# Moving band loads between two DMA queues in a convolution and involution kernel: SyncE issues every eighth transfer of a band instead of every fourth

## The chip, the cores and the metric

The kernel runs on one core of a Trainium2 chip. The metric is the device time of one execution in microseconds (us); lower is better. The kernel before took 1477.5 us in the median of three runs (1473.41 to 1481.04).

## What is computed

The input `x` has 32 images of 256 channels and 32 x 32 pixels, in float32. Two residual layers follow each other. The first adds a 3 x 3 convolution, rounded to half precision, of the group-normalized input. The second adds an involution: every pixel gets its own 7 x 7 weights for each of 16 groups of channels.

```python
# layer 0
x = x + conv3x3_fp16(gn(x), L0_conv_weight) + L0_conv_bias
# layer 1, with xn = gn(x)
y = relu(bn(einsum('oc,bchw->bohw', w1, xn)))        # 256 -> 64 channels
w = einsum('oc,bchw->bohw', w2, y) + b2              # 64 -> 7*7*16 weights per pixel
w = w.reshape(b, 16, 49, 32, 32)
patches = all 7x7 shifts of the padded xn, as (b, 16, 16, 49, 32, 32)
out = einsum('bgkhw,bgckhw->bgchw', w, patches)
x = x + out.reshape(b, 256, 32, 32)
```

## The kernel before

The kernel goes image by image, in steps that one hand-written loop lays out: 16 steps per image, and at each step the loop emits some work of several images at different stages. The order in which an engine's instructions are emitted is the order in which it runs them. The order is the same for the queues of DMA transfers, which SyncE (SP) and GpSimd (POOL) issue.

An image passes these stages.

- `load_x` (L105, SP) brings the image in. `front` does the group norms on ScalarE (L210, L269), the 3 x 3 convolution on TensorE (L320), its addition on VectorE (L334, L336), the 256 to 64 reduction (L368, L375) and the transposed pixels (L383, L387).
- `weights` makes the involution weights of four image rows: TensorE multiplies into `pw` (L398), and VectorE adds the bias and writes the result into the ring `w_sb` (L416). The ring holds 24 rows (`RING`), so a row's place is written again 24 rows later, and VectorE then has to wait until the scatter of the old rows has read them.
- `scatter` (L465, SP) copies a band of eight rows out of `w_sb` into the scratch `wd` in HBM, as seven transfers of 160 KB, one for each horizontal shift.
- `load_bands` (L478) reads the same band back in another layout, into one of three SBUF buffers (`bands`, `NBAND`), as 16 transfers of 70.2 KB. Each fills eight partitions of the buffer.
- `sums` (L503) multiplies the band with the transposed pixels on TensorE, and `add_windows` (L519) adds the result to the image on VectorE. `store` (L524, SP) writes the image out.

An image has four bands (`K`), so there are 128 bands, 896 scatter transfers and 2048 band loads. In the step loop, the scatter of a band stands one or two bands' worth of steps ahead of its load, and the load stands nine steps ahead of its sums. Within a step the scatter is emitted before the band load. On SP's queue the order is therefore: scatter of band k+1, loads of band k, scatter of band k+2, loads of band k+1, and so on, with the image's two loads and two stores in between.

Each queue has eight semaphores in rotation. A transfer waits for the one that was issued eight places earlier on the same queue, besides what its data need: a scatter waits for VectorE's writes and for the loads of the band that last used its rows of `wd`; a band load waits for the scatter of its band and for the sums that last used its buffer.

Which queue issues which of a band's 16 loads is decided by this line and the constant `SHARE`:

```python
queue = nc.sync if i % SHARE == SHARE - 1 else nc.gpsimd
queue.dma_start(band[j::JC, :, j * WB : j * WB + WPIX], src)
```

With `SHARE = 4`, SP issues the loads 3, 7, 11 and 15 of a band, and POOL the other twelve. POOL has nothing else to do after the start.

Of the kernel before, what the change touches and what calls it, by code (L numbers as in the profile page):

```python
# [59 lines left out]
ROW = S * WPIX  # L60
WR = 4
NBAND = 3
SHARE = 4
NPIX = 6
RING = 24
FRONT = -56
# [5 lines left out]
def tile_quant_conv_then_involution(  # L72
# [394 lines left out]
    def load_bands(b, k):  # L467

        band = bands[(b * K + k) % NBAND]
        for i in range(JC):  # L470
# [5 lines left out]
            )  # L476
            queue = nc.sync if i % SHARE == SHARE - 1 else nc.gpsimd
            queue.dma_start(band[j::JC, :, j * WB : j * WB + WPIX], src)  # L478
# [136 lines left out]
```

## Time and profile before

| | |
|---|---|
| median of 3 runs | 1477.5 us |
| profiled execution | 1467.2 us |
| its span, first to last instruction | 1465.4 us |
| mean granted clock of TensorE | 0.961 |
| TensorE busy | 1296.1 us |
| VectorE busy | 931.2 us |
| GpSimd busy, issue of its transfers included | 863.6 us |
| ScalarE busy | 734.7 us |
| moved by DMA | 369.32 MB, 252 GB/s in the mean |

The profile is that of one execution, so its parts add up to that execution's time and not to the median. A row of the groups names the line, the engine, the operation and the tiles; then it gives the busy time and the mean of one instruction, and the idle time of the engine ahead of it with what ended that idle time. A row of the waits reads "engine line waited for <- releaser: us in total, times, longest us". SP and POOL appear as SPq and POOL where they issue transfers. Queue q1 is the one that SP fills, and q0 the one that POOL fills.

### The profile page before, as it was taken

To read this page: it belongs to the slowest core of one execution; us is meant where nothing else is said; L and a number is where in the kernel's file an instruction comes from. 1 tells how busy PE (TensorE), PEld (TensorE's weight loads), DVE (VectorE), ACT (ScalarE), POOL (GpSimd) and SP (SyncE) were. 2 spreads that over 40 slices of the span, in tenths; PEclk is the share of its full clock that TensorE was granted. 3 is DMA by queue.
4 is the path that set the end of the run, shared out by engine and by line. 5 is a ranking of instruction groups with operands and counts; after the bars stand their busy time and mean duration, and the time that the engine had idled before them with its cause. 6 is when DMAs were issued, how large, how long until landed. Compare 5 with 4: busy or idle time off the path is not lost.

```text
span 1465.4 us, 70178 instructions
## 1 busy us (share of the span) xinstructions
PE 1296.1 (88%) x29440; PEld 804.8 (55%) x29440; DVE 931.2 (64%) x3180; ACT 734.7 (50%) x1699; POOL 863.6 (59%) x1561
## 2 busy tenths in 40 slices
PE   4899989898989899889898989998999999899764
PEld 1455555565556565556565555565555555556553
DVE  4566666676666676666666656666666666666652
ACT  5865545554545545455554555554555545553300
POOL 6066656565655566555566556566655556566664
PEclk9999999999999999999999999999999999999886
DMA  6189999999999999999999999999999999999996
GB/s 205 23 229 272 259 261 271 262 269 249 266 256 259 265 263 265 263 256 259 262 265 249 262 261 263 258 263 256 263 268 260 260 266 265 265 264 252 271 262 194
DMA packets 360089, 369.32 MB, mean 252 GB/s; under 512 B 72480, under 2 KB 302048, under 8 KB 359520
## 3 DMA queue, kind: packets, MB, share of 16 engines
q1 hardware_dynamic: 286048, 254.14, 61.9%
q0 software_dynamic: 73728, 110.69, 28.6%
q8 instruction: 235, 3.85, 1.1%
q14 instruction: 78, 0.64, 0.1%
HBM read 183.81 MB, written 180.74 MB: 249 GB/s over the span
## 4 chain that ended last, share of the span: by engine, by line
PE 42%; DMA 30%; SPq 10%; DVE 8%; issue 5%; ACT 3%; POOL 2%; DVEq 0%; ACTq 0%; POOLq 0%
PE pc L320 18%; DMA wd<-w_sb 14%; DMA band<-wd 14%; PE acc L503 11%; PE pw L398 9%; SPq L465 8%; DVE w_sb L416 5%; PE py L368 3%; POOL band L478 2%; DMA out<-x 2%; PE pt L383 1%; SPq L478 1%; ACT junk L210 1%; DVE x L519 1%; DVE x L336 1%
## 5 line engine op out<-in xcount | busy, mean ns | idle before, releaser
L478 POOL DMA_DIRECT2D band<-wd x1536 | 838.2, 548 | 588.3 <-DMA band<-wd 405.1
L416 DVE TENSOR_TENSOR w_sb<-pw,b_sb 128x16 f32<-128x16 f32 (+9 forms) x1920 | 454.2, 349 | 446.9 <-PE pw L398 269.5
L320 PE MATMUL pc<-xq,wq 128*128 128x496 f16 (+3 forms) x2304 | 550.0, 386 | 28.7 <-ACT xq L269 21.4
L503 PE MATMUL acc<-band,pixels 64*32 64x190 f32 (+1 forms) x16384 | 414.1, 321 | 40.9 <-issue 14.7
L320 PEld LDWEIGHTS <-wq 128*128 128x128 f16 x2304 | 210.1, 100 | 338.5 <-issue 130.6
L398 PE MATMUL pw<-w_sb,y 64*32 64x224 f32 (+1 forms) x8192 | 313.8, 340 | 87.9 <-DVE w_sb L416 61.0
L503 PEld LDWEIGHTS acc<-band,pixels 64*32 64x32 f32 x16384 | 295.7, 107 | 126.6 <-issue 79.7
L519 DVE TENSOR_TENSOR x<-acc,x 128x380 f32<-128x380 f32 (+1 forms) x512 | 261.7, 511 | 33.1 <-PE acc L503 24.2
L398 PEld LDWEIGHTS pw<-w_sb,y 64*32 64x32 f32 x8192 | 182.9, 108 | 141.1 <-issue 115.5
L210 ACT ACTIVATE junk<-x 128x512 f16<-128x512 f32 (+1 forms) x192 | 146.8, 764 | 74.9 <-DVE x L336 69.6
L387 ACT COPY pixels<-pt 128x512 f32<-128x512 f32 x128 | 73.6, 575 | 193.7 <-PE pt L383 193.7
L210 ACT ACTIVATE junk<-x,mean 128x1024 f16<-128x1024 f32 x128 | 147.1, 1149 | 4.3
L241 ACT ACTIVATE s<-back,eps 128x2 f32<-128x2 f32 x64 | 18.9, 296 | 201.0 <-DVE back L226 200.9
L334 DVE TENSOR_SCALAR q<-pc 128x512 f16<-128x512 f32 x128 | 87.3, 682 | 16.9 <-PE pc L320 16.8
L269 ACT ACTIVATE xn<-x,off,rstd 128x512 f32<-128x512 f32 x128 | 96.1, 799 | 0.0
L336 DVE SCALAR_TENSOR_TENSOR x<-q,bias_sb,x 128x512 f32<-128x512 f16 x128 | 91.9, 718 | 0.2
L231 ACT ACTIVATE mean<-back 128x2 f32<-128x2 f32 x64 | 12.9, 202 | 143.1 <-DVE back L226 143.1
L383 PE MATMUL pt<-ident,xn 128*128 128x128 f32 x512 | 77.8, 275 | 3.5 <-ACT pixels L387 3.5
L383 PEld LDWEIGHTS pt<-ident,xn 128*128 128x128 f32 x512 | 63.8, 142 | 29.9 <-ACT pixels L387 4.4
L269 ACT ACTIVATE xq<-x,off,rstd 128x1024 f16<-128x1024 f32 x64 | 75.9, 1228 | 2.3 <-PE pc L320 2.3
L368 PEld LDWEIGHTS py<-xn,w_sb 128*64 128x64 f32 x2048 | 63.1, 138 | 18.9 <-issue 13.6
L368 PE MATMUL py<-xn,w_sb 128*64 128x64 f32 x2048 | 68.0, 224 | 3.2 <-ACT xn L269 1.8
(40 smaller groups left out, 370.7 us busy)
## 6 DMA issues: line engine op xcount, KB each, us to landing
wd<-w_sb SPq DMA_DIRECT2D x896, 160.0 KB
band<-wd POOLq DMA_DIRECT2D x1536, 70.2 KB
band<-wd SPq DMA_DIRECT2D x512, 70.2 KB
x<-in_x SPq DMA_DIRECT2D x64, 512.0 KB
out<-x SPq DMA_DIRECT2D x64, 512.0 KB
band<-in_w SPq DMA_DIRECT2D x2, 1152.0 KB
w_sb<-in_w SPq DMA_DIRECT2D x2, 196.0 KB
wd<-band SPq DMA_DIRECT2D x2, 180.0 KB
```

Source lines behind the costliest of these rows:

```text
L210: nc.scalar.activation(junk[:, n0:n1], src[:, h, n0:n1], func, bias=bias, accum_out=self.sums[:, i : i + 1])
L269: nc.scalar.activation(dst, src, AF.Identity, bias=self.off[:, one], scale=self.rstd[:, one])
L320: nc.tensor.matmul(pc.rearrange("p (r c) -> p r c", c=W)[:, r0 - nt * RT : r1 - nt * RT, c0:c1], wq[:, kh, k, mh * P : (mh + 1) * P], xq[: ...
L336: nc.vector.scalar_tensor_tensor(xt[:, mh, cols], q, bias_sb[:, mh : mh + 1], xt[:, mh, cols], ALU.add, ALU.add)
L368: nc.tensor.matmul(py[i * CR : (i + 1) * CR, cols], w1_sb[:, kh, :], px[:, r : r + 2], start=kh == 0, stop=kh == CH - 1,)
L383: nc.tensor.transpose(pt[:, i, h * P : (h + 1) * P], xn[:, h, (m + i) * P : (m + i + 1) * P], ident)
L398: nc.tensor.matmul(pws[i][t * TW : (t + 1) * TW, r, : dj.stop - dj.start], y_sb[b % 2][half, (r0 // 2 + r) * W : (r0 // 2 + r + 1) * W], w ...
L416: nc.vector.tensor_tensor(to, pws[i][:p, r : r + rows, e, d0 * G : d1 * G].rearrange("p r (d g) -> p r d g", g=G), b2_sb[:p, e, d0 * G : d ...
L465: nc.sync.dma_start(to, rows.rearrange("p s g r -> p s (g r)"))
L478: queue.dma_start(band[j::JC, :, j * WB : j * WB + WPIX], src)
L503: nc.tensor.matmul(at[t * TW : (t + 1) * TW, h, :, f - top : l - top], px[p, a, v * GC : v * GC + TW], of[:, :, 2 * a + v, f - top : l - top],
L519: nc.vector.tensor_tensor(x_at, of, x_at, ALU.add)
```

## The change

The constant is doubled, and nothing else is edited.

```diff
-SHARE = 4
+SHARE = 8
```

SP now issues the loads 7 and 15 of a band, and POOL the other fourteen. Over the 128 bands SP issues 256 band loads instead of 512, and POOL 1792 instead of 1536. The transfers themselves are the same: same source, same destination and same size.

## The prediction

> **What bounds the kernel now.** I read the page's part 1 and 2 first, then the queues, the chain, the waits of the steady part (130 to 1390 us), and last the order of time on SyncE's queue.
>
> ```profile
> PE 1296.1 (88%) x29440; PEld 804.8 (55%) x29440; DVE 931.2 (64%) x3180; ACT 734.7 (50%) x1699; POOL 863.6 (59%) x1561
> ...
> DMA  6189999999999999999999999999999999999996
> ...
> q1 hardware_dynamic: 286048, 254.14, 61.9%
> q0 software_dynamic: 73728, 110.69, 28.6%
> ...
> PE 42%; DMA 30%; SPq 10%; DVE 8%; issue 5%; ACT 3%; POOL 2%; DVEq 0%; ACTq 0%; POOLq 0%
> ```
>
> No engine is full: PE is busy 88% of the span and 1152.1 of the 1260 us between 130 and 1390, so it idles 107.9 us there. The transfer engines are at 0.95 in the same stretch, and the chain gives DMA and SP's queue 40% together. The waits of that stretch say where PE's idle time comes from:
>
> ```profile
> POOL band L478 <- DMA band<-wd: 379.8, 277, 9.5
> DVE w_sb L416 <- PE pw L398: 246.9, 176, 5.9
> ...
> DVE w_sb L416 <- DMA wd<-w_sb: 95.4, 19, 8.4
> ...
> DVE w_sb L416 <- DMA band<-wd: 64.7, 13, 7.2
> ...
> PE pw L398 <- DVE w_sb L416: 57.1, 42, 4.4
> POOL band L478 <- DMA wd<-w_sb: 54.4, 23, 6.2
> ...
> PE pw L398 <- issue: 25.4, 26, 2.2
> ```
>
> VectorE (L416) writes new weights into the ring w_sb and must first see that the scatter (L465) has taken the old ones out. 32 times, about once an image, it waits 5.0 us on average (95.4 + 64.7 = 160.1 us). By the instruction list the DMAs that L416 waits for are scatters only; the name band<-wd in the second row is that of the update that came last. PE then waits for VectorE: 57.1 us, the largest cause of its idle time. PE waits for a band itself only 13.2 us in the whole run.
>
> Why is the scatter late? SP's queue in order of time (start, length, instructions):
>
> ```profile
> 817.02 5.28 SPq L465 DMA_DIRECT2D wd<-w_sb  x7
> 822.41 2.68 SPq L478 DMA_DIRECT2D band<-wd  x4
> 825.45 5.02 SPq L465 DMA_DIRECT2D wd<-w_sb  x7
> 830.57 3.54 SPq L478 DMA_DIRECT2D band<-wd  x4
> 834.21 0.40 SPq L524 DMA_DIRECT2D out<-x  x1
> 834.97 6.04 SPq L465 DMA_DIRECT2D wd<-w_sb  x7
> 841.10 1.63 SPq L524 DMA_DIRECT2D out<-x  x1
> 842.83 2.72 SPq L478 DMA_DIRECT2D band<-wd  x4
> ```
>
> There is hardly a hole. Summed over 130 to 1390 us from the trace's records, SP spends 595.1 us issuing scatters (813, mean 732 ns), 332.7 us band loads (466, mean 714 ns), 70.9 us image loads and stores: 998.7 us, 79% of the stretch; most of the rest waits for a free slot, because each transfer waits for the one issued eight before it on the same queue. Pairing each scatter with the VectorE instruction that it waits for, I find that the scatter goes out 5.1 us (median) after its data are ready. So **SP's queue is late by its own issuing**, not for want of data.
>
> **What the Trainium skill says.** "DMA: Bandwidth & Descriptors", section "Issuing engines are not separate DMA queues": transfers of all issuers run on the same 16 engines, and spreading them saves only the time to initiate. The trace agrees that this time counts: 714 ns each on SP, 547 on POOL. Same page, "Why a DMA increments its semaphore by 16 and not by 1": a transfer whose outer dimension is 8 runs on 8 engines; from SP on the lowest eight, from POOL on eight chosen by a rotating cursor, and from POOL all 16 post. The trace agrees in part: a band load on SP shows one update about 1.0 us after its issue and eight more at 3.7 to 5.2 us, one on POOL shows 16; and the first scatter behind four band loads has eight of its updates within 0.36 us, the other eight spread out to 2.0 us. So SP's band loads do pile on one half of the engines; the cursor is not visible here. "SBUF — State Buffer", section "SBUF: two separate sides", warns that VectorE in some modes stops POOL from writing descriptors. This trace shows none of it: 1536 issues on POOL took 547 ns in the minimum and the median, 681 at most.
>
> **The change part by part.** Sizes, sources and waits for data stay; per band SP issues 2 loads instead of 4, POOL 14 instead of 12.
>
> (1) *Off SP:* 256 issues x 713 ns = 183 us, with the gaps ahead of them (72.6 us for 466 in the steady part, 0.156 us each) 256 x 0.87 = 222 us, or 7 us per image. This lies on the path: the next scatter stands right behind the loads. It comes 2 x 0.87 = 1.7 us earlier at once, and more as the queue stops carrying lateness over from band to band. I take 3 us of the 5.1 as recovered (bounds: 1.7 and 5.1). VectorE's wait of 5.0 us falls to 2.0, and PE's 57.1 us shrink in the same ratio: -57.1 x 3/5 = **-34 us** (bounds -19 and -57; with the 25.4 us of unexplained idle time at L398 -82).
>
> (2) *Onto POOL:* 256 x 547 ns = 140 us of issuing. POOL too has eight slots. Its 12 loads take 7.8 us from first to last issue (0.71 each), and it idles 2.5 us on average before the next band. 14 loads make 9.2 + 0.5 = 9.7 us plus about 0.2 us of start against a band period of 43.3/4 = 10.8 us: it still fits, at 92%. Scatters land unevenly, though (8.9, 9.1, 10.6 and 15.4 us apart), so the four bands of an image end later by about 1.7, 2.5, 4.2 and 2.9 us. The cover is the time between the last POOL landing and the start of the sums: medians 3.2, 3.7, 4.9 and 8.0 us. Subtracting band by band, PE would lose 1.04 us per image, 33 us in all, if the scatters came no earlier. But POOL starts 0.8 us after the scatter lands, so the 3 us of (1) go straight off its delays, leaving at most 1.2 us, inside the cover: I take **+2 us** (bounds 0 and +33).
>
> (3) *Engines of the DMA:* each moved load has 32 small packets of 10 ns instead of 8: 256 x 24 x 10 ns / 16 = 4 us of engine time; I take **+2 us**. Against it, SP's band packets hold 2002 us of engine time on eight engines, 250 us each. Half of it moved and spread evenly takes 125 - 62.5 = 62 us from the fuller eight. How much of it reaches the end the trace of before cannot show (bounds 0 and -62); I count 0 here, since it is partly the same gain as (1).
>
> (4) *SP's remaining waits:* scatter k waits for POOL's loads of band k-4 and POOL for the sums of band k-3 (12 us in all now, PE pt); both have room of ten us and more, so later POOL loads cost nothing there, unless POOL falls a whole band behind.
>
> Sum: -34 + 2 + 2 = -30 us. The profiled execution took 1467.2 us (span 1465.4 and 1.8 around it), so 1437, or 0.98 of it. The median of the three runs is 1477.5, 0.7% above the profiled one; I take the same 30 us from it: **1447**.
>
> **The rivals.**
> *A, POOL becomes the late queue (slower).* Place: L478 on POOL. At 14 loads per band it is 92% occupied, and a band that starts behind keeps the lateness until the 15 us gap of the fourth. It decides where the scatters land less than about 1 us earlier than now. Price: +33 us by (2), 1510. For it: POOL's 379.8 us of slot waits, the largest line. Against: POOL's rest of 2.5 us per band, and 5.1 us of lateness upstream that mends. 16%.
> *B, nothing moves (same).* The bytes are the same and the DMA engines are 0.95 busy; a queue that issues earlier only waits longer in the engines. For it: latencies of 5.2 to 5.9 us in both queues point to full engines. Against: periods per image vary from 39 to 47 us at the same bytes, and the engines' share falls to 0.92 in some stretches. 1470 to 1485; 14%.
> *C, the uneven halves are the true limit (faster by more).* Then the whole 62 us of (3) come off: 1415. For it: the eight late updates behind the band loads. Against: PE, 91% busy in the steady part, could not follow all the way. 15%.
> That the change doesn't do what it says is excluded: the instruction lists of the two kernels differ by the queue of these 256 loads and, following from it, in which earlier transfer a later one on either queue waits for; PE, VectorE and ScalarE have the same order in both.
>
> **How the numbers follow.** My own case, 55%, gives 1425 to 1468 (its bounds of -19 to -57, with a few us each way). Cases of faster are it and C, 0.70; B 0.14; A 0.16. The lines of faster and slower stand 0.5% (7.4 us) from 1477.5, about what measurements of this kernel can tell from no change. The range leaves out the ends of A and C: 1413 to 1492.
>
> **What would show it.** In the profile after: SP's queue with holes, the scatter issued about 2 us after its data instead of 5; the two L416 waits for DMAs well under 160 us; PE pw L398 <- DVE w_sb near 25 us; PE's share of the span at 90%; POOL near 1004 us busy (863.6 + 140). Step (2) is wrong if PE's wait for the bands at L503 rises from 13 us to 30 or more. The whole forecast is wrong if L416 waits for scatters as long as now although SP's queue has holes: then the landing, not the issue, was slow.

## The result, and the profile after

The kernel after takes **1413.2 us** in the median of four runs (1408.4 to 1422.0), the kernel before 1476.5. The ratio is 0.9576, with a 95% interval of [0.9518, 0.9634]. Beside the last experiments it was measured again: 1411.0 us and a ratio of 0.9574, [0.9536, 0.9612]. So 4.2% are gone, twice the 2.0% of the forecast. The direction and most of the mechanism were right; the size was not.

The page of the profiled execution (1416.5 us, span 1414.7), in the parts that were shown of before:

```profile
PE 1265.2 (89%) x29440; PEld 802.2 (57%) x29440; DVE 933.0 (66%) x3180; ACT 729.8 (52%) x1699; POOL 1003.5 (71%) x1817
...
DMA  6099899999999999999999999999999999999995
...
q1 hardware_dynamic: 279904, 235.72, 57.2%
q0 software_dynamic: 86016, 129.14, 34.5%
...
PE 47%; DMA 31%; issue 7%; POOL 5%; DVE 4%; ACT 3%; SPq 2%; POOLq 0%; DVEq 0%; ACTq 0%
```

SP's queue falls from 10% of the chain to 2%, and POOL rises from 2% to 5%. TensorE's busy time is 31 us shorter (1296.1 before), although it does the same work. The waits of the steady part, 130 to 1340 us here:

```profile
DVE w_sb L416 <- PE pw L398: 333.8, 214, 4.8
POOL band L478 <- DMA band<-wd: 229.0, 294, 2.9
...
PE acc L503 <- DMA band<-wd: 17.8, 13, 3.2
...
DVE w_sb L416 <- DMA wd<-w_sb: 11.2, 3, 6.1
...
DVE w_sb L416 <- DMA band<-wd: 4.1, 1, 4.1
...
PE pw L398 <- DVE w_sb L416: 1.0, 3, 0.5
```

VectorE's waits for the scatter fall from 160.1 us to 15.3, and TensorE's wait behind them from 57.1 us to 1.0. Now VectorE waits for TensorE instead (333.8 us). SP's queue in order of time:

```profile
780.74 5.01 SPq L465 DMA_DIRECT2D wd<-w_sb  x7
785.85 2.10 SPq L478 DMA_DIRECT2D band<-wd  x2
790.12 5.52 SPq L465 DMA_DIRECT2D wd<-w_sb  x7
795.73 1.79 SPq L478 DMA_DIRECT2D band<-wd  x2
...
806.03 1.46 SPq L478 DMA_DIRECT2D band<-wd  x2
811.02 1.18 SPq L105 DMA_DIRECT2D x<-in_x  x2
```

There are holes of 2.2 us (787.95 to 790.12) and 3.5 us (807.49 to 811.02). The scatter goes out 1.2 us (median) after its data are ready, against 5.1 before.

What the prediction did not have is in the granted clock, the share of its full speed at which TensorE is allowed to run. The first two views are of before, its mean clock and TensorE's order of time; the last is the mean clock of after:

```profile
core 0: 1465.4 us, clock 0.961
```

```profile
327.79 2.08 PE L320 MATMUL pc<-xq,wq 128*128 128x512 f16 x9
329.80 1.52 PE L503 MATMUL acc<-band,pixels 64*32 64x190 f32 x64
335.57 0.54 PE L398 MATMUL pw<-w_sb,y 64*32 64x224 f32 x2 [4.26 <-DVE w_sb L416]
336.57 2.00 PE L398 MATMUL pw<-w_sb,y 64*32 64x224 f32 x30 [0.47 <-DVE w_sb L416]
338.50 2.67 PE L320 MATMUL pc<-xq,wq 128*128 128x496 f16 x9
```

```profile
core 0: 1414.7 us, clock 0.978
```

TensorE stands still for 4.26 us, because VectorE waits for a scatter. When it starts again, 30 multiplications into `pw` take 2.00 us, where 32 take 1.05 us elsewhere, and nine of L320 take 2.67 us instead of the 2.08 of the first row. The trace's clock record has an episode, a stretch at half clock, from 336.3 us on, 3.4 us long. Before has 25 such episodes with 117.4 us in all, after 12 with 64.9 us. The difference lies between 130 and 1340 us, where before has 15 with 71.7 us and after 6 with 20.5 us. All of these 21 begin inside a gap of at least 1 us in TensorE's work or within 4 us of its end. In before 13 of the 15 stand at a gap in which TensorE waited for VectorE at L398, in after none of the 6. Not every gap has an episode: of the 26 gaps of 1 to 2 us in that part of before 7 have one, of the 12 longer ones 10. That the clock differs is not a matter of one profile: its mean is 0.976 to 0.983 in the eight executions of after, and 0.953 to 0.970 in those of before that stood beside all the experiments.

### The profile page after: what moved, and what is told of

The parts are those of the page before. It is cut to its first block, busy times and chain, and to the rows that moved or that the text cites. A ratio compares the mean times of both kernels' runs of the same rounds, so it can differ in the third digit from the quotient of the medians.

```text
span 1414.7 us, 70076 instructions
## 1 busy us (share of the span) xinstructions
PE 1265.2 (89%) x29440; PEld 802.2 (57%) x29440; DVE 933.0 (66%) x3180; ACT 729.8 (52%) x1699; POOL 1003.5 (71%) x1817
## 4 chain that ended last, share of the span: by engine, by line
PE 47%; DMA 31%; issue 7%; POOL 5%; DVE 4%; ACT 3%; SPq 2%; POOLq 0%; DVEq 0%; ACTq 0%
DMA band<-wd 24%; PE pc L320 19%; PE acc L503 15%; PE pw L398 9%; DMA wd<-w_sb 7%; POOL band L478 5%; PE py L368 3%; DVE w_sb L416 2%; PE pt L383 2%; SPq L465 2%; ACT junk L210 1%; DVE x L519 0%; DVE w_sb L147 0%; ACT xn L269 0%; DVE q L334 0%
## 5 line engine op out<-in xcount | busy, mean ns | idle before, releaser
L478 POOL DMA_DIRECT2D band<-wd x1792 | 978.0, 548 | 397.8 <-DMA band<-wd 249.0
L320 PE MATMUL pc<-xq,wq 128*128 128x496 f16 (+3 forms) x2304 | 536.5, 379 | 31.3 <-ACT xq L269 21.4
L503 PE MATMUL acc<-band,pixels 64*32 64x190 f32 (+1 forms) x16384 | 420.5, 323 | 78.9 <-DMA band<-wd 39.6
L503 PEld LDWEIGHTS acc<-band,pixels 64*32 64x32 f32 x16384 | 298.3, 108 | 171.1 <-issue 101.5
L320 PEld LDWEIGHTS <-wq 128*128 128x128 f16 x2304 | 206.4, 98 | 328.9 <-issue 114.6
L398 PE MATMUL pw<-w_sb,y 64*32 64x224 f32 (+1 forms) x8192 | 296.6, 333 | 31.1 <-issue 29.4
L398 PEld LDWEIGHTS pw<-w_sb,y 64*32 64x32 f32 x8192 | 182.8, 107 | 63.0 <-issue 43.9
L383 PEld LDWEIGHTS pt<-ident,xn 128*128 128x128 f32 x512 | 64.0, 142 | 27.4 <-issue 3.2
L383 PE MATMUL pt<-ident,xn 128*128 128x128 f32 x512 | 78.1, 275 | 0.9 <-ACT pixels L387 0.9
L368 PEld LDWEIGHTS py<-xn,w_sb 128*64 128x64 f32 x2048 | 63.0, 139 | 16.5 <-issue 8.1
L368 PE MATMUL py<-xn,w_sb 128*64 128x64 f32 x2048 | 67.8, 224 | 2.3 <-ACT xn L269 1.8
## 6 DMA issues: line engine op xcount, KB each, us to landing
band<-wd POOLq DMA_DIRECT2D x1792, 70.2 KB
band<-wd SPq DMA_DIRECT2D x256, 70.2 KB
```

Of the source, the lines that this page charges most:

```text
L320: nc.tensor.matmul(pc.rearrange("p (r c) -> p r c", c=W)[:, r0 - nt * RT : r1 - nt * RT, c0:c1], wq[:, kh, k, mh * P : (mh + 1) * P], xq[: ...
L368: nc.tensor.matmul(py[i * CR : (i + 1) * CR, cols], w1_sb[:, kh, :], px[:, r : r + 2], start=kh == 0, stop=kh == CH - 1,)
L383: nc.tensor.transpose(pt[:, i, h * P : (h + 1) * P], xn[:, h, (m + i) * P : (m + i + 1) * P], ident)
L398: nc.tensor.matmul(pws[i][t * TW : (t + 1) * TW, r, : dj.stop - dj.start], y_sb[b % 2][half, (r0 // 2 + r) * W : (r0 // 2 + r + 1) * W], w ...
L503: nc.tensor.matmul(at[t * TW : (t + 1) * TW, h, :, f - top : l - top], px[p, a, v * GC : v * GC + TW], of[:, :, 2 * a + v, f - top : l - top],
```

## The experiments

Two theories stood against each other. **Theory 1**: SyncE's queue was late by its own issuing, so scatters were late, VectorE waited for the ring and TensorE for VectorE. **Theory 2**: band loads from SyncE pile on eight of the 16 DMA engines, and the change evened the halves. Kernels that were measured together ran on the same chip, beside the kernel before.

### Two loads to ScalarE's queue (e1_act_two)

The edit is shortened to the line that chooses the queue; it starts from the kernel before.

```diff
-            queue = nc.sync if i % SHARE == SHARE - 1 else nc.gpsimd
+            # loads 3 and 11 of a band, five steps later; SHARE = 4
+            queue = nc.scalar if late else nc.sync if i % SHARE == SHARE - 1 else nc.gpsimd
```

> The two loads of a band that the change took from SyncE (3 and 11) are issued by ScalarE's queue, five steps later in the loop; SyncE has 2 as in the kernel after, GpSimd has 12 as in the kernel before, and all four loads that GpSimd doesn't issue still use eight engines. Theory 1 (SyncE's issuing made the scatter late, and this alone was worth the 63 us): about 1415, within 15 us, the L416 waits for scatters under 40 us, with some cost of ScalarE's issuing. Theory 2 (the uneven halves of the DMA engines, relieved by GpSimd's rotation): 1465 or more, since the halves are as uneven as before.

Measured: 1461.1 us, ratio 0.9959 [0.9924, 0.9995]. This does not decide between them. In this program ScalarE's transfers use the same eight semaphores as SyncE's, so that each queue can wait for the other's. SyncE waits longer than in before (64.4 us for the first of these rows there, 1.1 us for the second), and ScalarE's norms wait too (130 to 1380 us; lines from L478 on have moved by two):

```profile
SPq L105 <- DMA out<-x: 98.1, 27, 5.0
SPq L465 <- DMA x<-in_x: 73.0, 42, 3.6
```

```profile
ACT xn L269 <- DMA band<-wd: 65.7, 19, 7.1
...
DVE w_sb L416 <- DMA wd<-w_sb: 53.8, 17, 6.7
PE acc L505 <- DMA band<-wd: 40.1, 20, 4.2
...
PE pw L398 <- DVE w_sb L416: 11.5, 20, 2.1
...
DVE w_sb L416 <- DMA band<-wd: 11.4, 2, 9.0
```

The scatter was still 4.0 us behind its data (5.1 before). VectorE's waits for it fell to 65.2 us all the same, and TensorE's wait at L398 from 57.1 to 11.5 us; but TensorE now waits 40.1 us for bands, and is at half clock for 109.9 us. Less lateness brings nothing where another wait takes its place.

### Two tiny transfers in place of the loads taken away (e2_tiny, e5_tiny16)

Both do extra work that nothing reads. The edits are shortened.

```diff
             queue.dma_start(band[j::JC, :, j * WB : j * WB + WPIX], src)
+            if i % 8 == 3:      # SHARE = 8 as after
+                nc.sync.dma_start(scratch[:8, :, at : at + 2], ...)     # e2: 128 bytes
+                nc.sync.dma_start(scratch[:16, 0, at : at + 2], ...)    # e5 has this one instead
```

> The kernel after, with two transfers of 128 bytes to an unused tile on SyncE's queue per band, where loads 3 and 11 stood before: SyncE issues as many transfers as before and they take its slots, but hardly a byte more moves and the halves stay as even as in the kernel after. Theory 1 (SyncE's issuing): most of the gain is lost, 1455 to 1490. Theory 2 (uneven halves): 1413 to 1425. If each has a share, the time lies between and the distances give the shares.

> As the kernel with two tiny transfers per band, but each tiny transfer fills 16 partitions instead of 8 and so runs on 16 engines. It takes a slot of SyncE's eight as before; what SyncE needs to issue it should be less (transfers on 16 engines took from 178 ns, those on 8 never under 567 ns). Theory 1a (SyncE's time for issuing decides): part of the gain comes back, 1430 to 1455. Theory 1b (the slots decide): no better than the kernel with 8 partitions, 1465 to 1480.

Measured: 1471.4 us, ratio 0.9988 [0.9962, 1.0014], and 1461.8 us, ratio 0.9949 [0.9924, 0.9975]. Two transfers that move next to nothing take away all the gain, or all but half a per cent of the time, while the halves stay even: in e5 the first scatter behind the loads has its updates spread over 1.5 us (2.0 before), the ninth 0.04 us after the eighth (0.32 before). Theory 2 falls: with as many issues on SyncE's queue as before, even halves bring no more than that half per cent. Of e2 only the time is used here. Waits of e5 (130 to 1340 us), which has the lines of `scratch` added and so other line numbers:

```profile
DVE w_sb L417 <- DMA wd<-w_sb: 95.4, 20, 9.8
...
PE pw L399 <- DVE w_sb L417: 60.5, 35, 4.5
...
DVE w_sb L417 <- DMA band<-wd: 55.5, 11, 9.1
```

They are close to those of before (95.4, 57.1 and 64.7 us). Theory 1a and 1b, time of issuing or slots, are not told apart: on 16 engines a tiny transfer was no cheaper to issue, against what was expected (0.78 us in the mean of e5, its band loads on 8 engines 0.70).

### More and fewer loads on SyncE (e4_share5, e3_share16)

```diff
-SHARE = 8
+SHARE = 5      # e4: loads 4, 9, 14 on SyncE
+SHARE = 16     # e3: load 15 on SyncE
```

> SyncE issues 3 loads of a band (4, 9, 14), GpSimd 13. Theory 1: SyncE stands between 79% and 74% issuing, the scatter is late by some 3 us and some L416 waits are left, GpSimd has more rest: 1415 to 1440. Theory 2: half way between the two kernels, about 1445.

> SyncE issues 1 load of a band, GpSimd 15. Theory 1: SyncE's scatters are already in time with 2, so nothing more is won there; GpSimd's queue, at 9.6 us from first to last issue of 14 and 0.3 us of rest in the kernel after, gets 0.73 us more per band and sets the pace: 128 x 0.5 to 0.7 us = 60 to 90 us more, 1475 to 1500. Theory 2: a further quarter of the unevenness goes, 1413 minus up to 31 us, 1385 to 1413.

| loads of a band on SyncE | 4 (before) | 3 (e4) | 2 (after) | 1 (e3) |
|---|---|---|---|---|
| ratio to before | 1 | 0.9657 | 0.9576 | 0.9967 |
| interval | | 0.9608 to 0.9706 | 0.9518 to 0.9634 | 0.9944 to 0.9990 |
| scatter issued after its data, median us | 5.1 | 2.9 | 1.2 | 0.04 |
| last band load landed ahead of its sums, median us | 4.2 | 3.4 | 1.4 | 0.6 |

The two lower rows are read from one profile each; a second profile of the kernel after has 0.3 us of lateness and 1.8 us for the loads. The row of lateness falls to nothing while the time goes up again. With one load left, GpSimd issues 15 and its bands come too late. The waits of e3 (130 to 1380 us):

```profile
PE acc L503 <- DMA band<-wd: 59.4, 37, 4.4
PE acc L503 <- issue: 30.4, 34, 2.6
```

That is rival A of the prediction, one step further on than it was feared. Theory 2 is wrong on both: its 1445 for e4 was 1418.1, and where it had a further gain for e3, nearly all of the gain was lost (1469.1). Theory 1's 1475 to 1500 for e3 was a little too high.

### Relief of SyncE without touching the band loads (e6_xpool, e14_load60)

Both start from the kernel before.

```diff
-            nc.sync.dma_start(xt[:, h], x[b, h * P : (h + 1) * P])
+            (nc.gpsimd if b else nc.sync).dma_start(xt[:, h], x[b, h * P : (h + 1) * P])   # e6
-LOAD = -63
+LOAD = -60                                                                             # e14
```

> The kernel before (SyncE 4 loads of a band, GpSimd 12), but the images after the first are loaded by GpSimd. SyncE loses two issues per image and the 2.4 us that it waits for a store's slot ahead of them: about 3.5 us per image, half of what the change took off it; the halves of the DMA engines stay as uneven as before. Theory 1 (SyncE's lateness): 1420 to 1450. Theory 2 (uneven halves): no change, 1465 to 1480.

> The kernel before with the image loads three steps later in the loop (LOAD -60 for -63). No transfer changes its queue; SyncE no longer waits for the store of the image whose buffer is taken (64.8 us in the steady part of the kernel before, 2.4 per image), while each image still arrives four steps before it is used. Theory 1: a third of the relief of the change (2.4 against 7 us per image), 1440 to 1462. Theory 2: no change, 1465 to 1478. If the wait was only a pause in which SyncE would have waited for slots anyway: no change either.

Measured: 1442.4 us, ratio 0.9822 [0.9791, 0.9853], and 1456.1 us, ratio 0.9871 [0.9833, 0.9909]. Both lie where theory 1 put them. e14 changes no transfer's queue, and its scatters still go out 2.3 us after their data instead of 5.1. It also shows where such a gain is lost again (130 to 1340 us):

```profile
ACT junk L210 <- DMA x<-in_x: 123.9, 36, 9.2
...
PE py L368 <- ACT xn L269: 82.1, 41, 5.9
...
DVE w_sb L416 <- DMA wd<-w_sb: 13.5, 6, 3.4
DVE w_sb L416 <- DMA band<-wd: 12.1, 6, 3.0
...
PE pw L398 <- DVE w_sb L416: 0.8, 2, 0.5
```

The stall at L398 is gone as in the kernel after, but TensorE now waits 82.1 us for ScalarE's norm at L368, 1.8 us in the whole kernel before. The first row says why: ScalarE waits 123.9 us for the image at the start of its norms, 0.3 us in the same part of before. So the image arrives too late now, which the expectation had ruled out. The half clock moved along: 14 of the 15 episodes in this part stand at a gap at L368.

### The stall of VectorE alone (e11_dve_delay)

The DMA queues are those of after; VectorE only fills an unused tile.

```diff
+        for _ in range(11 if r0 == 4 else 0):
+            nc.vector.memset(idle, 0.0)
         for i in range(2):
             for e in range(2):
                 p = P if e == 0 else (K1 // 2) * TW
```

> The kernel after, with 11 fills of an unused tile on VectorE (4.7 us in all, by the 0.84 ns per element of the one fill in the trace) once per image, ahead of the weight additions of the second group of rows, where VectorE waited 5.0 us for scatters in the kernel before. The DMA queues are those of the kernel after. Theory 1 in full (VectorE's wait, TensorE's stall behind it, and half-clock episodes of TensorE after the stall make the difference between the two kernels): 1445 to 1475, with TensorE's waits at L398 for VectorE back at some 57 us and the time at half clock between 90 and 120 us instead of 65. If a stall of TensorE costs only its own length, the half-clock time stays at 65 us and the time at 1430 to 1445. If VectorE's rest (34% of the span) takes it up: under 1425.

Measured: 1453.7 us, ratio 0.9858 [0.9798, 0.9918]. TensorE's waits and the clock in its profile (line numbers moved by the added lines):

```profile
PE pw L399 <- DVE w_sb L419: 57.7, 53, 3.2
PE acc L506 <- issue: 17.2, 23, 2.0
```

```profile
core 0: 1457.1 us, clock 0.962
```

With 4.7 us of fills per image in the one place, and 1.5 us between them, TensorE waits 57.7 us as before (57.1), it is at half clock for 112.2 us (before 117.4, after 64.9), and 40 of the 63 us are back (by the ratios 2.8 of the 4.2%). Of the 17 episodes between 130 and 1340 us 16 stand at a gap in which TensorE waited for VectorE at L399. Most of what the stall costs is not its length. TensorE's gaps come to 130.8 us against 125.4 in the kernel after, since those ahead of the sums shrink from 78.4 to 43.1 us, while 47.3 us more are at half clock, which at full clock would have taken half of that. Another 5.5 us of this profile's span lie ahead of the first multiplication and belong to neither.

### Further settings (e7_mixed, e8_share5_xpool, e12_share5_xact, e13_mixed_load60, e15_after_again)

The first edit is shortened. e7, e8, e12 and e13 start from the kernel after.

```diff
+            share = 5 if k in (0, 3) else SHARE      # e7 and e13: 3, 2, 2, 3 loads on SyncE
-LOAD = -63
+LOAD = -60                                           # e13 too
+SHARE = 5      # e8 with the image loads on GpSimd, e12 with them on ScalarE
```

> SyncE issues 3 loads of an image's first and fourth band and 2 of the second and third, because it waits for data ahead of the scatters that follow those two. GpSimd issues 13 and 14. Theory 1: both queues are in time, 1395 to 1413, or the same as the kernel after if neither of them sets the pace there any more. Theory 2: worse than the kernel after, about 1430.

> SyncE issues 3 loads of a band and no image loads after the first, GpSimd 13 loads of a band and the image loads. Theory 1: SyncE is relieved about as far as in the kernel after (5.25 + 3.5 us per image against 7), GpSimd gets half a transfer per band more than with 13 loads and less than with 14: 1400 to 1420. Theory 2: about 1445.

> SyncE issues 3 loads of a band and no image loads after the first; ScalarE issues those, GpSimd 13 loads of a band. Theory 1: SyncE gives up 3.5 us per image against the kernel with 3 loads alone, and GpSimd has a load less per band than in the kernel after: 1390 to 1412, if ScalarE (half idle) is not held up by the slots of the image loads; 1420 or more if it is.

> 3, 2, 2, 3 loads of an image's four bands on SyncE, and the image loads three steps later. SyncE's wait for the store (88.5 us in the steady part of the kernel with 3, 2, 2, 3 alone) goes. Theory 1: the scatters come out with their data, 1390 to 1408; if GpSimd's queue or TensorE sets the pace by now, 1405 to 1415 as before.

> The kernel after, again, beside the others of this call: 1405 to 1420, a ratio to the kernel before of 0.956 to 0.966.

Measured: e7 1411.5 us, ratio 0.9602 [0.9560, 0.9643], not to be told from the kernel after, although its scatters go out 2.4 us after their data; it has 6.6 us of waiting at L398 and 59.1 us at half clock. Theory 1 was wrong about this kernel's queues and right about its time. e8 1445.4 us (0.9841 [0.9793, 0.9889]): its scatters are in time (0.03 us median) and yet 25 us are missing to the top of what was expected. GpSimd's band loads wait 99.1 us for the slots of the image loads (130 to 1340 us), and TensorE 25.9 us for bands. e12 1502.5 us (1.0183 [1.0127, 1.0240]), slower than before: ScalarE stands still ahead of the image loads, and TensorE waits 94.5 us for it at L383 (130 to 1380 us):

```profile
ACT pixels L387 <- DMA out<-x: 125.6, 12, 11.8
...
PE pt L383 <- ACT pixels L387: 94.5, 27, 6.0
```

e13 1435.4 us (0.9729 [0.9705, 0.9752]) lies 20 us above the higher of its two expectations: lateness is nearly gone (0.04 us), but TensorE's idle time rises by 25 us against e7, of which the waits show 16.6 us for the norm at L368 and 21.5 us more at L398 without a named cause. As in e14, ScalarE waits for the image (60.1 us). What holds TensorE at L398 stays open. The kernel after again, e15, came out as expected, 1411.0 us and 0.9574. No kernel beat the one after beyond its interval. Lateness alone does not tell the time: e7 and e4 are late by 2.4 and 2.9 us and fast, e8 and e13 are in time and slower.

## Why the prediction had half of the gain

TensorE's time can be taken apart in each profile (us): its gaps between the first and the last multiplication, its time at half clock, and its busy time less half of that, an estimate of what the same work takes at full clock. The 24 to 30 us that are missing to the span stand ahead of the first multiplication and behind the last.

| profile | span | gaps | half-clock time | busy less half of that |
|---|---|---|---|---|
| before | 1465.4 | 145.0 | 117.4 | 1237.4 |
| after | 1414.7 | 125.4 | 64.9 | 1232.8 |
| e11, stall added | 1457.1 | 130.8 | 112.2 | 1240.7 |
| e5, tiny transfers | 1451.9 | 137.1 | 124.5 | 1228.2 |
| e4, 3 loads | 1425.6 | 123.9 | 53.1 | 1245.5 |
| e3, 1 load | 1459.8 | 165.8 | 84.7 | 1227.6 |

The last column stays within 1228 and 1246 here; two runs that are not in the table lie lower (e12 1221.8, e14 1217.0), so that small shares cannot be read from it. From before to after the gaps give 19.6 us, the clock (117.4 - 64.9)/2 = 26.2 us, the rest 4.6 us: 50.4 of the 50.7 us of the two spans. The clock's share is an estimate. TensorE also stands still in some of its half-clock time; it is busy in 93.2 us of it before and in 49.7 after, and by these the clock gives 21.8 us.

**Step (1), off SP: right in mechanism, mis-sized.** SP's lateness fell to 1.2 us, not to the assumed 2.1, and the wait at L398 to 1.0 us, not to 23: 56 us instead of 34, at the upper bound that was named (57). SP's own relief was smaller than forecast. In the steady part its issuing fell from 34.4 to 30.6 us per image, by 3.8 us and not by the 5.7 of 183 us over 32 images, because the issues that stayed took longer: band loads 862 ns in the mean against 714, scatters 767 against 732. The step's sum took TensorE's wait as its whole price. **This is the term that failed**: the half-clock episodes at these gaps were put at nothing. That they went is worth 22 to 26 us, by the two estimates above, which no step counted. Steps (1) and (2) together forecast 32 us fewer gaps, and 19.6 us came; it is the clock that carries the gain beyond the forecast. e11 shows the clock's part with the queues left alone.

"TensorE: Matmul & The Clock Gate" of the Trainium skill, section "Part 1: The HAM clock gate", says that TensorE falls to half rate after an idle window of some 3.4 us and comes back after a busy one. The trace agrees in the length of the episodes (3.4 us or multiples) and in that they stand at gaps. It differs in the length of the gap: 9 of the 15 episodes of before between 130 and 1340 us have no gap of 3 us beside them, such as the one at 418.2 us, behind a gap of 2.2 us, and of the 17 of e11 none has.

**Step (2), onto POOL: +2 was too low.** POOL is busy 1003.5 us as forecast (1004). But its rest ahead of a band falls from 2.5 to 0.3 us, and the landing from 4.2 to 1.4 us ahead of the sums. TensorE's idle time at L503 rises from 40.9 to 78.9 us, that for bands from 13.2 to 39.6 us, beyond the mark of 30 that the prediction set. The +38 us lie above the upper bound of +33. With the -56 of step (1) they make -18, close to the 19.6 us by which all gaps together fell: what was mis-sized in (1) and in (2) largely cancels.

**Step (3), engines of the DMA: 0 for the halves was right** by e2 and e5, though the halves did become even. Behind the loads, the scatter's ninth update came 0.32 us after the eighth before and 0.07 us after. Rival C had the right time, 1415, for the wrong reason. That the measured 1413.2 still lies in the forecast range of 1413 to 1492 is luck: its lower end made room for C, and the forecast's own case ended at 1425. **Step (4)** holds: in the waits of after POOL waits 0.5 us for PE pt.

**Rival A** does not decide at 14 loads, where it costs the 38 us of step (2), but at 15. **Rival B** falls: the engines are still 0.97 busy in the steady part of after, moving 274 GB/s instead of 262. A high busy share was no proof of a full resource.

The profiled execution of before (1467.2 us) was faster than all four that were timed (1473.4 to 1481.0); against the medians, 63 us are gone, against the profiles 51. The 17 us by which e11 stays below the kernel before that was measured beside it (1470.4) are not explained.

## What to carry to other kernels

A queue that only issues can be what the others wait for. Pair each transfer with the work that makes its data, and see how long after it the transfer goes out; then move or drop issues ahead of it, whatever their size. A stall of TensorE should be priced with the half-clock stretch at its gaps, and less the waits that it hides elsewhere; and a queue that takes over the work should be checked for the point at which its own results come late: here one load of sixteen lay between the best time and hardly any gain.

## What was not expected of the hardware

In e5 a transfer of 128 bytes on 16 engines took SyncE 0.78 us to issue in the mean, a band load of 70.2 KB on 8 engines 0.70 us, and a scatter of 160 KB 0.75 us: in these means the time hardly depends on what is moved. It is no constant of the transfer either: with fewer loads on its queue SyncE took longer for each (862 ns in after, 714 in before); why is not shown. The tiny transfers also took 4.9 us in the mean from issue to their last update, against 4.3 us for the band loads beside them.
